# A graph and mixer block with routed experts: counts laid out by node, the mixer's sums taken over normalised x, the search before the statistics, the experts' tiles in the table's place

## Chip, cores and metric

The kernel runs on 1 core of one Trainium2 chip. The metric is the device time of the whole program in microseconds (us). Before the change it is 1842.44 us, the median of 4 runs (1831.82 to 1848.07).

## The reference, cut to what matters

```python
edge_index = jnp.stack([src, dst])                    # 200,000 edges, sorted by dst; 6,250 nodes, 256 channels
xn = _layernorm(x, axis=-1)
x = x + _L0_gnn_ref(edge_index, xn, W, b) \
      + _L0_mix_ref(xn[None], Wqkv, ln1_g, ln1_b, W1, b1, W2, b2, ln2_g, ln2_b)[0]
x = x + _L0_ffn_ref(_layernorm(x, axis=-1)[None], gate_w, gate_b, w1, b1, w2, b2)[0]

# _L0_gnn_ref: relu( sum over edges of (xn @ W)[src] * dinv[src] * dinv[dst], summed by dst, with self loops, + b )
# _L0_mix_ref: linear attention, 8 heads of 32
q, k = elu(q) + 1, elu(k) + 1
kv   = einsum('nshd,nshm->nhmd', k, v);  ksum = sum(k, axis=1)
z    = 1 / (einsum('nlhd,nhd->nlh', q, ksum) + 1e-6)
t    = einsum('nlhd,nhmd,nlh->nlhm', q, kv, z)
x1   = layer_norm(t + x) ; y = W2 gelu(W1 x1 + b1) + b2 ; layer_norm(y + x1)
# _L0_ffn_ref: softmax gate, top 1 of 8 experts, 977 slots per expert,
#              relu(h @ w1 + b1) @ w2 + b2, times the gate's probability
```

## The kernel before, in words

P is 128 and nodes are handled in NB = 49 tiles of 128 rows (the last has 106). The program has three stages, and the order of instructions on each engine is written out by hand in the first two: generators yield, and a loop takes turns between them.

**First stage.** Two generators alternate, `first_passes` (F) and `first_chain` (C); F may take FIRST = 0.79 steps for each step of C. Before the loop, the statistics of the first eight tiles of x are taken (`all_of(x_stats(8))`).
- C begins with `search()` (L424): 25 comparisons `lt` of the sorted dst list with node numbers, each with two matmuls into `et_ps` (L436), give a rough position for every eighth node; windows `er` of dst are then fetched and counted to find where each node's edges begin. Then come the statistics of the rest of x, `graph_rows` (which writes the scaled x as the table `tab` in SBUF and as `g_dram` in DRAM), interleaved with `edge_lists` (per-edge lists `idx`, `hiT`, `loT`), and `checked()`, which sums violations of the layout's assumptions into `odd`.
- F runs the mixer's first half over 25 groups of two tiles: x is normalised (`normed`, L682), transposed on PE (`turned`, L242), multiplied with Wq (L708), and with Wk and Wv together (L721, one bank of 512 columns a tile); ACT takes exp and relu of q and k and copies v with a column of ones into `va` (L730). `outer` (L694) sums k^T [v, 1] of each head pair into `kv_ps` with 129 columns. q goes to `q_dram`. Each group also writes a part of `xbuf` with zeros (`blanks`). F yields five times a group.
- At the end `kv_ps` is masked into `kvb`, `odd` is summed, `badi` is read by all engines (L766), and a branch (L767) leads to a general path that these inputs do not take.

**Main loop** (L871 on). Three generators alternate, driven by the gather's steps:
- `gather()`: for 18 tiles of nodes (GTS), edges are fetched by an indirect DMA of 128 rows of `g_dram` into `gt` (L977, GB = 9 buffers, issued LAG = 7 steps before use), and a matmul with a one-hot matrix `oh` sums them by node (L995).
- `dense()`: for the other 31 tiles (DTS; one of them called a block u), one-hot matrices `lo` and `hi` of the edges (DVE, L899) are multiplied on PE (L963) into counts `bp`: for each node pair of a step, 98 columns, how many edges go to it from each of the 49 source tiles. ACT casts the counts to bytes (L965) into `A`, laid out as [source row, source tile s, node]; 13 steps (NS) fill one A. In the block after, A is cast by source tile to `A_r` (L926; two buffers, four or five source tiles in each of 12 steps) and multiplied with the table, `ps_d` (L952). The sum goes through `put_sum` (L886).
- `rounds()`: for each group of two tiles the attention's result, the two layer norms, the MLP, the gate and the routing, in steps spread over three groups a, b and c; the norms run on ACT at L1199 with `nb` and `rs` from DVE's chain of small instructions (L222 to L1193). The tokens' rows go to `xbuf` by indirect DMA (L1076): 256 channels normalised, 256 as residual, the gate's probability and the row number, ROW = 514 floats.

**Experts** (L1307 on). For each of 8 experts `prepare` loads `w1e`, `w2e` and the expert's rows `xe` from `xbuf`, all issued on SP, and transposes them; `group` multiplies (L1360, L1370), scales by the probability `xe[:, i, 512]`, adds the residual and scatters rows to `out`. Its tiles are in a pool of their own, opened after the main loop's pools close.

The code before the change, where the two counts' casts stand:

```python
                s0, s1 = share(p)
                o = parts[p] = de.tile([P, 5, P], FR, name="A_r", tag="A_r")
                nc.scalar.copy(o[:, :s1 - s0, :], mats[u][:, s0:s1, :])
...
                        nc.scalar.copy(mats[u][:, :, GN * g0:GN * g1].rearrange("p s (g k) -> p g s k", k=GN),
                                       bp[:, :(g1 - g0) * HI].rearrange("p (g s k) -> p g s k", g=g1 - g0, k=GN))
```

Of the kernel before, what the change touches and what calls it, by code (L numbers as in the profile page):

```python
# [7 lines left out]
F32 = mybir.dt.float32  # L8
# [43 lines left out]
GB = 9  # L52
LAG = 7
# [3 lines left out]
FIRST = 0.79  # L57
# [12 lines left out]
def graph_block_kernel(  # L70
# [36 lines left out]

    main = ExitStack()
# [4 lines left out]
    big = main.enter_context(tc.tile_pool(name="big", bufs=1))  # L113
# [202 lines left out]
    vas = []  # L316
    for i in range(2):
        va = raw.tile([P, 2, 129], F32, name=f"va{i}")
        V.memset(va[:, :, 128:129], 1.0)
        vas.append(va)  # L320
# [32 lines left out]
    kv_ps = kps.tile([P, 2, 132], F32, name="kv_ps")  # L353
    cr_ps = rps.tile([P, 512], F32, name="cr_ps")
    sm_ps = rps.tile([P, 512], F32, name="sm_ps")
# [147 lines left out]
    def edge_lists():  # L503
# [38 lines left out]
        def ask(c):  # L542
            if c < NGC:
                got[c] = [rw.tile([P, P], I32, name=o, tag=o) for o in ("gd", "gs")]
                fetch(got[c], gsi[:, c:c + 1])
            elif c < NGC + NDC:
                d = 2 * (c - NGC)
                got[c] = [rw.tile([P, 2, P], I32, name=o, tag=o) for o in ("wd", "ws")]
                for h in range(2):
                    fetch([w[:, h, :] for w in got[c]], ei[:, d + h:d + h + 1])  # L550
# [28 lines left out]
        for c in range(NDC):  # L579
# [12 lines left out]
            V.scalar_tensor_tensor(kf, hs, float(GN), kf, op0=OP.mult, op1=OP.add)  # L592
# [70 lines left out]
    def first_passes():  # L663
# [11 lines left out]
        def normed(gi):  # L675
# [3 lines left out]
            xn = pair("S", 2, "xn")  # L679
            for i in range(n):  # L680
                v = xts[gi][:r, i, :] if gi >= NX else x_in(t0 + i, 1)[:, 0, :]
                nc.scalar.activation(xn[:r, i, :], v, AF.Identity,  # L682
# [9 lines left out]
        def outer(t, r, ek, va):  # L692
            for g in range(2):
                nc.tensor.matmul(kv_ps[:, g, :129], ek[:r, g * P:(g + 1) * P], va[:r, g, :],  # L694
                                 start=(t == 0 and g == 0), stop=(t == NB - 1 and g == 1))

        turned(0, normed(0))
        yield
        for gi in range(NGR):
# [12 lines left out]
            re = pair("G", 3, "re")  # L712
            nc.scalar.activation(re[:, :, :nn], qp[:, :, :nn], AF.Relu)
            xn = normed(gi + 1) if gi + 1 < NGR else None
            yield
            V.scalar_tensor_tensor(ex[:, :, :nn], ex[:, :, :nn], 1.0, re[:, :, :nn], op0=OP.min, op1=OP.add)
            nc.sync.dma_start(q_dram[gi, :, :, :nn], ex[:, :, :nn])
            for i in range(n):
                kp = bank()
                for c in range(2):  # L720
                    nc.tensor.matmul(kp[:r, :], xnt[:, c, i * r:i * r + r], wqkv_s[:, c, D:3 * D],  # L721
                                     start=(c == 0), stop=(c == 1))
                if late:
                    outer(*late.pop())
                ek = rw.tile([P, D], F32, name="ek", tag="ek", bufs=2)
                nc.scalar.activation(ek[:r], kp[:r, :D], AF.Exp)
                rk = rw.tile([P, D], F32, name="rk", tag="rk", bufs=1)
                nc.scalar.activation(rk[:r], kp[:r, :D], AF.Relu)
                va = vas[i]
                nc.scalar.copy(va[:r, :, 0:128], kp[:r, D:].rearrange("p (g m) -> p g m", g=2))  # L730
                yield
                V.scalar_tensor_tensor(ek[:r], ek[:r], 1.0, rk[:r], op0=OP.min, op1=OP.add)
                if i == 0 and xn is not None:
                    turned(gi + 1, xn)
                late.append((t0 + i, r, ek, va))
                yield
# [5 lines left out]
    with tc.manual_schedule():  # L742
        all_of(x_stats(8))
        F, C = first_passes(), first_chain()
        f = c = 0
        live = [True, True]
        while any(live):
            if live[1]:
                live[1] = next(C, "end") != "end"
                c += 1  # L750
            while live[0] and (f < FIRST * c or not live[1]):
                live[0] = next(F, "end") != "end"
                f += 1
        for g in range(2):
            V.tensor_tensor(kvb[:, g, 0:128], kv_ps[:, g, 0:128], hmask.rearrange("p a b -> p (a b)"), op=OP.mult)
            V.tensor_scalar(kvb[:, g, 128:132], hmask[:, :, 0], kv_ps[:, g, 128:129], None, op0=OP.mult)
# [5 lines left out]
        V.tensor_scalar(badi, bad, 0.5, None, op0=OP.is_gt)  # L762
    rwx.close()


    flag = nc.values_load(badi[0:1, 0:1], min_val=0, max_val=1)  # L766
# [102 lines left out]


    with tc.tile_pool(name="ga", bufs=GB, side="right") as ga, \  # L871
# [42 lines left out]
        def dense():  # L914

            mats, parts = {}, {}
            acc_ps = None

# [3 lines left out]
            def widened(u, p):  # L922

                s0, s1 = share(p)
                o = parts[p] = de.tile([P, 5, P], FR, name="A_r", tag="A_r")
                nc.scalar.copy(o[:, :s1 - s0, :], mats[u][:, s0:s1, :])  # L926
# [15 lines left out]
            for u in range(ND + 1):  # L942
                for p in range(NS):
                    k = u * NS + p
                    if u >= 1 and p >= 1:
# [4 lines left out]
                        A, (s0, s1) = parts.pop(p), share(p)  # L950
                        for hi in range(s0, s1):
                            nc.tensor.matmul(acc_ps, A[:, hi - s0, :], source(hi), start=False, stop=(hi == NB - 1))  # L952
                    make(k + 2)
                    if u < ND and p == 0:
                        mats[u] = de.tile([P, NB, P], U8, name="A", tag="A")
                    if u >= 1 and p < NS - 1:
                        widened(u - 1, p + 1)
                    if u < ND:
# [3 lines left out]
                        for g in range(g1 - g0):  # L962
                            nc.tensor.matmul(bp[:, g * HI:(g + 1) * HI], lo[:, g, :], hi[:, g, :],  # L963
                                             start=(g == 0), stop=(g == g1 - g0 - 1))
                        nc.scalar.copy(mats[u][:, :, GN * g0:GN * g1].rearrange("p s (g k) -> p g s k", k=GN),  # L965
                                       bp[:, :(g1 - g0) * HI].rearrange("p (g s k) -> p g s k", g=g1 - g0, k=GN))
# [116 lines left out]
        def rounds():  # L1083
# [3 lines left out]
            order = [NGR - 1] + list(range(NGR - 1))  # L1087
            xts, qs, ss, slots = {}, {}, {}, {}
# [4 lines left out]

            def load(k):
                if k < NGR:
                    gi = order[k]
                    t0, n = twos[gi]
                    r = rows(t0)
                    xts[gi] = pair("X", 3, "xt")
                    nc.sync.dma_start(xts[gi][:r, :n, :], node_rows(x, t0, n))  # L1100
                    qs[gi] = pair("Q", 2, "q")
                    nc.sync.dma_start(qs[gi][:, :, :n * r], q_dram[gi, :, :, :n * r])
# [11 lines left out]
            load(0)  # L1114
            yield
            for k in range(-2, NGR):
# [70 lines left out]
                if a is not None:  # L1187
                    load(k + 3)
# [104 lines left out]
        j = 0  # L1293
        while any(alive.values()):
# [4 lines left out]
            while alive["s"] and done_s < SIDE * (j + 1):  # L1299
                step("s", S)  # L1300
                done_s += 1
            j += 1
# [4 lines left out]
    with tc.tile_pool(name="fw", bufs=2) as fw, tc.tile_pool(name="fc", bufs=1) as fc, \  # L1307
# [14 lines left out]
        def prepare(e):  # L1322

            w1e = fw.tile([P, 2, DFF], F32, name="w1e", tag="w1e")
            nc.sync.dma_start(w1e, fw1[e].rearrange("(c p) f -> p c f", p=P))
            w2e = fw.tile([P, DFF // P, D], F32, name="w2e", tag="w2e")
            nc.sync.dma_start(w2e, fw2[e].rearrange("(c p) d -> p c d", p=P))
            xe = fw.tile([P, NCT, ROW], F32, name="xe", tag="xe")
            r0 = e * CAP
            for i0, i1 in ((0, 4), (4, NCT - 1)):  # L1330
                nc.sync.dma_start(xe[:, i0:i1, :],
                                  xbuf[r0 + i0 * P:r0 + i1 * P, :].rearrange("(t p) d -> p t d", p=P))
            nc.sync.dma_start(xe[:last, NCT - 1, :], xbuf[r0 + (NCT - 1) * P:r0 + CAP, :])
# [110 lines left out]
```

## Time and profile before

| | us |
|---|---|
| median of 4 runs | 1842.44 (1831.82 to 1848.07) |
| the profiled execution, whole | 1833.91 |
| its span, first to last instruction | 1832.0 |
| PE busy | 1495.7 (82%) |
| ACT busy | 1112.7 (61%) |
| DVE busy | 1087.6 (59%) |
| POOL busy | 775.3 (42%) |
| mean granted clock of TensorE | 0.919 |
| DMA | 286.43 MB, 156 GB/s over the span |

PE is the matmul unit, PEld its weight loads, DVE the vector engine, ACT the scalar engine, POOL GpSimd, SP the engine that issues most DMAs. "L952" is line 952 of the kernel. In a line of groups the name before the arrow is the tile written, those after it the tiles read; then shape, count, busy time, mean ns of one, and the idle time of the engine just before it with what ended it. In the order of time each line has start, duration, engine, line, tile, count and in brackets the idle time before it and its releaser. In a line of waits come the total, the number of times and the longest. Durations of pipelined instructions overlap, so the time from start to next start is the one that adds up.

### The profile page before, as it was taken

The numbers are of one execution on the slowest core, as the hardware profiler recorded it, in microseconds if no ns is written. First come the engines' busy times: TensorE is split into PE (matmuls) and PEld (weight loads), VectorE is DVE, ScalarE is ACT, GpSimd is POOL, SyncE is SP. The second block draws the span as 40 slices with busy tenths as digits, with TensorE's granted clock in tenths as the row PEclk, the third lists the DMA queues.
The fourth block names the chain that finished last, engine by engine and source line by source line (L and its number), as shares of the span: only waits on it lengthen the run. The fifth ranks groups of instructions, "written<-read, shape, count | busy, mean of one in ns | idle before, by whom it ended". The sixth has DMA issues, their size and how long they took to land. (4 is left out here: it accounts for less than half of the span.)

```text
span 1832.0 us, 23628 instructions
## 1 busy us (share of the span) xinstructions
PE 1495.7 (82%) x7678; PEld 1062.5 (58%) x7678; DVE 1087.6 (59%) x3430; ACT 1112.7 (61%) x1794; POOL 775.3 (42%) x771
## 2 busy tenths in 40 slices
PE   4887776888878888888788888877888649999997
PEld 2555454665556665556665565555666426777775
DVE  4765856675676677667676767666866412323323
ACT  1844656777676877677777777776777313233332
POOL 0104506556546565555565556555565311111111
PEclk9988996999989998989888999988999969999999
DMA  7546787666556666565666666655566462332330
GB/s 227 153 121 196 256 256 190 162 162 175 147 158 167 157 168 176 145 167 150 160 171 166 161 165 165 167 142 159 154 170 155 109 218 104 108 107 103 111 107 21
DMA packets 184987, 286.43 MB, mean 156 GB/s; under 512 B 28457, under 2 KB 78564, under 8 KB 184714
## 3 DMA queue, kind: packets, MB, share of 16 engines
q0 software_dynamic: 96304, 180.15, 37.7%
q1 hardware_dynamic: 88250, 103.44, 17.4%
q8 instruction: 70, 1.15, 0.3%
q10 hardware_dynamic: 288, 1.08, 0.1%
q14 instruction: 75, 0.61, 0.1%
HBM read 226.90 MB, written 60.39 MB: 157 GB/s over the span
## 5 line engine op out<-in xcount | busy, mean ns | idle before, releaser
L977 POOL DMA_INDIRECT gt<-g_dram,idxc x612 | 624.1, 1020 | 524.8 <-PE ps L995 298.0
L965 ACT CAST A<-bp 128x490 uint8<-128x490 f32 (+1 forms) x403 | 511.7, 1272 | 259.3 <-PE bp L963 116.6
L952 PE MATMUL ps_d<-tab,A_r 128*128 128x512 f32 x1519 | 468.0, 434 | 118.9 <-ACT A_r L926 92.2
L952 PEld LDWEIGHTS ps_d<-tab,A_r 128*128 128x128 f32 x1519 | 297.7, 205 | 224.1 <-ACT A_r L926 123.0
L995 PE MATMUL ps<-gt,oh 128*128 128x512 f32 x612 | 280.2, 492 | 9.4 <-DMA gt<-g_dram,idxc 8.8
L899 DVE TENSOR_TENSOR lo<-rowb,lo 128x640 bf16<-128x640 bf16 (+1 forms) x403 | 194.1, 482 | 126.7 <-PE bp L963 44.8
L926 ACT CAST A_r<-A 128x512 fp32r<-128x512 uint8 x372 | 251.5, 676 | 15.7 <-PE ps_d L952 5.7
L963 PEld LDWEIGHTS <-lo 128*128 128x128 bf16 x1984 | 107.7, 104 | 130.3 <-issue 65.4
L963 PE MATMUL bp<-hi,lo 128*128 128x98 bf16 x1984 | 168.9, 218 | 12.5 <-DVE hi L899 9.8
L1388 POOL DMA_INDIRECT out<-rep,who x43 | 42.5, 988 | 300.4 <-DVE rep L1386 201.9
L986 DVE TENSOR_TENSOR oh<-rowb,rel 128x256 fp32r<-128x256 bf16 x306 | 127.7, 418 | 68.7 <-PE ps L995 35.7
L899 DVE TENSOR_TENSOR hi<-hib,hi 128x490 bf16<-128x490 bf16 (+1 forms) x403 | 162.9, 404 | 0.0
L1360 PE MATMUL hpf<-xet,w1e 128*128 128x512 f32 (+2 forms) x544 | 151.5, 436 | 5.6 <-ACTq L1400 3.5
L1370 PE MATMUL ypf<-w2e,hm 128*128 128x256 f32 (+1 forms) x688 | 151.3, 379 | 0.0
L1370 PEld LDWEIGHTS ypf<-w2e,hm 128*128 128x128 f32 (+1 forms) x688 | 128.9, 188 | 21.9 <-issue 3.1
L995 PEld LDWEIGHTS ps<-gt,oh 128*128 128x128 f32 x612 | 114.9, 203 | 16.0 <-DMA gt<-g_dram,idxc 8.2
L1360 PEld LDWEIGHTS hpf<-xet,w1e 128*128 128x128 f32 x544 | 85.5, 191 | 65.3 <-issue 57.4
L1362 ACT ACTIVATE hm<-hpf,fb_s 128x512 f32<-128x512 f32 (+2 forms) x136 | 71.1, 526 | 78.3 <-PE hpf L1360 72.9
L1372 DVE TENSOR_TENSOR y<-ypf,fb_s 128x256 f32<-128x256 f32 (+1 forms) x43 | 18.2, 423 | 142.8 <-PE ypf L1370 142.8
L721 PE MATMUL mm<-wqkv_s,xnt 128*128 128x512 f32 (+1 forms) x196 | 97.7, 623 | 0.0
L1373 ACT ACTIVATE y<-y,xe 128x256 f32<-128x256 f32 (+1 forms) x43 | 21.8, 508 | 119.4 <-DVE y L1372 119.4
L1076 POOL DMA_INDIRECT xbuf<-slot,put x48 | 52.8, 1101 | 61.3 <-issue 50.5
(307 smaller groups left out, 2035.6 us busy)
## 6 DMA issues: line engine op xcount, KB each, us to landing
g_dram<-tab SPq DMA_DIRECT2D x24, 512.0 KB
xt<-in_x SPq DMA_DIRECT2D x42, 256.0 KB
xbuf<-zeros SPq DMA_DIRECT2D x26, 384.0 KB
gt<-g_dram,idxc POOLq DMA_INDIRECT x612
xe<-xbuf SPq DMA_DIRECT2D x8, 1028.0 KB
w1e<-in_fw SPq DMA_DIRECT2D x8, 1024.0 KB
w2e<-in_fw SPq DMA_DIRECT2D x8, 1024.0 KB
xe<-xbuf SPq DMA_DIRECT2D x8, 771.0 KB
```

Source lines behind the costliest of these rows:

```text
L721: nc.tensor.matmul(kp[:r, :], xnt[:, c, i * r:i * r + r], wqkv_s[:, c, D:3 * D], start=(c == 0), stop=(c == 1))
L899: V.tensor_tensor(one[:, :g1 - g0, :].rearrange("p g (w t) -> p g w t", t=2), row.rearrange("p (w t) -> p w t", t=2).unsqueeze(1).to_broad ...
L926: nc.scalar.copy(o[:, :s1 - s0, :], mats[u][:, s0:s1, :])
L952: nc.tensor.matmul(acc_ps, A[:, hi - s0, :], source(hi), start=False, stop=(hi == NB - 1))
L963: nc.tensor.matmul(bp[:, g * HI:(g + 1) * HI], lo[:, g, :], hi[:, g, :], start=(g == 0), stop=(g == g1 - g0 - 1))
L965: nc.scalar.copy(mats[u][:, :, GN * g0:GN * g1].rearrange("p s (g k) -> p g s k", k=GN), bp[:, :(g1 - g0) * HI].rearrange("p (g s k) -> p ...
L977: nc.gpsimd.indirect_dma_start(out=gt, out_offset=None, in_=g_dram, in_offset=bass.IndirectOffsetOnAxis(ap=idxs[j // IC][:, j % IC:j % IC ...
L986: V.tensor_tensor(oh, rowb.unsqueeze(1).to_broadcast([P, 2, P]), rel[:, m:m + 2].unsqueeze(2).to_broadcast([P, 2, P]), op=OP.is_equal)
L995: nc.tensor.matmul(ps, ohs.pop(i), tiles.pop(i), start=False, stop=(e == EB - 1))
L1360: nc.tensor.matmul(hp[:, :nn], w1e[:, c, f * P:(f + 1) * P], xet[:, c, at:at + nn], start=(c == 0), stop=(c == 1))
L1362: nc.scalar.activation(hm[:, f, :nn], hp[:, :nn], AF.Relu, bias=fb1_s[:, e * 8 + f:e * 8 + f + 1])
L1370: nc.tensor.matmul(yp[:r, :], hm[:, f, (i - i0) * P:(i - i0) * P + r], w2e[:, f, :], start=(f == 0), stop=(f == DFF // P - 1))
```

## The change

- **Counts by node.** `A` is laid out as [source row, node, source tile]. The cast of `bp` writes in a row; the cast to `A_r` reads with a step of 49 bytes, in chunks of CH = 7 source tiles (7 a block instead of 12).
- **GB and LAG** go from 9 and 7 to 8 and 6.
- **Mixer.** `xn` gets a column of ones and three buffers of its own; k is computed for both tiles of a group in one bank, with no v; `outer` sums k^T [xn, 1] with 257 columns into `kx_ps` (two banks). After the loop `kx` is copied, transposed and multiplied with Wv into kv, and then masked. `normed` runs two groups ahead. Three yields a group; FIRST is 0.465. `sm_ps` becomes a part of the bank of `cr_ps`.
- **Search ahead.** ALONE = 9 steps of C run before `all_of(x_stats(8))`.
- **Flag.** `judged()` sums `odd` when C ends, and `badi` is read two steps of F later; the branch stands where it stood.
- **Rounds' first loads** of x and q are issued before the branch.
- **Experts in the table's place.** The pool `big` of the tables stays open to the end. The experts' weights lie in T0 and T1, `xe` in T2 and T3, `hm` in T4 and T5. The first expert's weights are asked for as soon as gather and dense are through, while rounds still runs. `xe` has 512 columns; probability and row number come as `xm` by DMAs of their own; the first expert's first four tiles come one by one. Both halves of a transposed group are written before the copies.
- hi's index becomes node times 49 plus source tile: `kf * NB + hs` in place of `hs * GN + kf`.

```diff
-GB = 9
-LAG = 7
+GB = 8
+LAG = 6
...
+ALONE = 9
+FIRST = 0.465
...
-            V.scalar_tensor_tensor(kf, hs, float(GN), kf, op0=OP.mult, op1=OP.add)
+            V.scalar_tensor_tensor(kf, kf, float(NB), hs, op0=OP.mult, op1=OP.add)
...
-            for i in range(n):
-                kp = bank()
...
-                    nc.tensor.matmul(kp[:r, :], xnt[:, c, i * r:i * r + r], wqkv_s[:, c, D:3 * D],
+            kp = bank().rearrange("p (t o) -> p t o", t=2)
+            for i in range(n):
...
+                    nc.tensor.matmul(kp[:r, i, :], xnt[:, c, i * r:i * r + r], wqkv_s[:, c, D:2 * D],
...
+                    nc.tensor.matmul(kx_ps[:, g, :D + 1], ek[:r, i, g * P:(g + 1) * P], xns[gi % 3][:r, i, :],
...
+        for _ in range(ALONE):
+            next(C)
+        all_of(x_stats(8))
...
+                if not live[1]:
+                    badi = judged()
+                    asked = f + 2
...
+                if not live[1] and f == asked:
+                    flag = nc.values_load(badi[0:1, 0:1], min_val=0, max_val=1)
...
+        kx = pair("S", 2, "kx")
+        nc.scalar.copy(kx, kx_ps[:, :, :D])
...
+                nc.tensor.transpose(tp[:, (2 * c + g) * P:(2 * c + g + 1) * P], kx[:, g, c * P:(c + 1) * P], ident)
...
+                nc.tensor.matmul(kv[:, g * P:(g + 1) * P], kxt[:, c, g, :], wqkv_s[:, c, 2 * D + g * P:2 * D + (g + 1) * P],
...
+            CH = 7
...
+            def widened(u, c):
+                if 0 <= u < ND and c * CH < NB:
+                    o = parts[u, c] = de.tile([P, CH, P], FR, name="A_r", tag="A_r")
+                    nc.scalar.copy(o, mats[u][:, :, c * CH:(c + 1) * CH].rearrange("p n s -> p s n"))
...
-                        mats[u] = de.tile([P, NB, P], U8, name="A", tag="A")
-                    if u >= 1 and p < NS - 1:
-                        widened(u - 1, p + 1)
+                        mats[u] = de.tile([P, P, NB], U8, name="A", tag="A")
+                    if p >= 1:
+                        for hi in range(*share(p)):
+                            if hi and hi % CH == 0:
+                                widened(u - 1, hi // CH + 1)
...
+                        nc.scalar.copy(mats[u][:, GN * g0:GN * g1, :].rearrange("p n s -> p (n s)"), bp[:, :(g1 - g0) * HI])
+                    if p == NS - 1:
+                        widened(u, 0)
+                    if p == 0:
+                        widened(u - 1, 1)
...
+            if not (alive["g"] or alive["d"] or weights):
+                weights.append(weights_of(0))
...
-            xe = fw.tile([P, NCT, ROW], F32, name="xe", tag="xe")
+            xe = big.tile([P, NCT, 2 * D], F32, name="xe", tag=f"T{2 + e % 2}")
+            xm = fw.tile([P, NCT, 2], F32, name="xm", tag="xm")
...
-            hm = fw.tile([P, DFF // P, 512], F32, name="hm", tag="hm")
+            hm = big.tile([P, DFF // P, 512], F32, name="hm", tag=f"T{4 + len(hms) % 2}")
```

## The prediction

> **What bounds the kernel now.** I first cut the span into its stages with the busy time by stretch (columns: length; busy time and count for PE, PEld, DVE, ACT, POOL; granted clock; DMA share; GB/s).
>
> ```profile
> 0.00:276.00 276.00, 204.88 (x828) 129.39 (x828) 181.30 (x635) 142.99 (x367) 54.23 (x67) 0.93 0.65 201
> 276.00:1457.00 1181.00, 967.34 (x5462) 698.55 (x5462) 800.68 (x2513) 858.94 (x1212) 672.94 (x656) 0.91 0.61 161
> 1457.00:1499.00 42.00, 9.28 (x38) 7.10 (x38) 11.04 (x55) 3.12 (x7) 5.62 (x5) 0.59 0.57 199
> 1499.00:1832.00 333.00, 314.17 (x1352) 227.50 (x1352) 94.60 (x228) 107.64 (x210) 42.50 (x43) 0.99 0.28 96
> ```
>
> The main loop is 1181 of 1832 us, and no engine fills it: PE 82%, ACT 73%, DVE 68%, POOL 57%. The experts are PE throughout (94%). So I next asked, for 300 to 1420, whom PE waits for, and then for ACT's groups by shape:
>
> ```profile
> PE ps_d L952 <- ACT A_r L926: 86.9, 45, 7.8
> ```
>
> ```profile
> L965 ACT CAST A<-bp 128x490 uint8<-128x490 f32 x359 | 463.3, 1290 | 230.1 <-PE bp L963 99.7 <-remote 62.7 <-PE ps L995 55.1
> L926 ACT CAST A_r<-A 128x512 fp32r<-128x512 uint8 x330 | 220.9, 669 | 0.6
> L926 ACT CAST A_r<-A 128x640 fp32r<-128x640 uint8 x29 | 22.4, 771 | 0.0
> ```
>
> PE and ACT wait for each other in turn. The order of time shows how:
>
> ```profile
> 833.67 0.63 ACT L926 CAST A_r<-A 128x512 fp32r<-128x512 uint8 x1
> 834.19 1.30 ACT L965 CAST A<-bp 128x490 uint8<-128x490 f32 x1
> ...
> 834.36 1.20 PE L952 MATMUL ps_d<-tab,A_r 128*128 128x512 f32 x4
> ...
> 838.36 1.09 ACT L1199 ACTIVATE s<-s,nb,rs 128x256 f32<-128x256 f32 x2 [2.86 <-DVE nb L1193]
> ...
> 840.34 0.60 ACT L926 CAST A_r<-A 128x512 fp32r<-128x512 uint8 x1
> ...
> 840.99 2.08 PE L952 MATMUL ps_d<-tab,A_r 128*128 128x512 f32 x4 [4.89 <-ACT A_r L926]
> ```
>
> The next A_r is queued on ACT behind two layer norms (838.36 to 840.34), the first of which waits 2.86 us for DVE; PE idles 4.89 us and then runs four matmuls in 2.08 us instead of 1.20, at a clock of 0.50 from 841 to 845.
>
> **Counts by node.** *Cast.* It read 490 floats and wrote pairs of bytes 128 apart; from start to next start it takes about 1.02 us (830.49 to 831.51). Now it writes 490 bytes in a row, as A_r does now: 0.52 us a 512 (833.67 to 834.19), slope (771-669)/128 = 0.80 ns an element, so 0.50 us. *Widening.* 7 chunks of 896 a block instead of 12 of about 512, each element now read 49 bytes on. In a row 896 would take 0.52 + 384 x 0.80 = 0.83 us; what the step adds, no ACT row shows. The cast bounds it above: its write lost 0.52 us on 490 elements, 1.06 ns an element or 2.12 ns a jump (245 jumps). The nearest read is on DVE, 256 bytes a step:
>
> ```profile
> L428 DVE CAST lastf<-dl x1: 186/186/186, 22.1 to 22.1; 125x25 f32<-125x25 int32 x1
> ```
>
> ```profile
> L493 DVE COPY begin<-cr_ps x1: 210/210/210, 105.5 to 105.5; 128x49 f32<-128x49 f32 x1
> ```
>
> ```profile
> L528 DVE COPY picked<-sm_ps x2: 169/172/175, 147.8 to 149.1; 128x16 f32<-128x16 f32 x2
> ```
>
> 16 and 49 elements in a row take 172 and 210 ns, so 25 would take 182; the strided read took 186, 0.16 ns an element more. A gain below a row of 0.83 us is excluded: the count of elements is the same. So a chunk takes 0.97 (DVE's price), 1.78 (the write's mean) or 2.73 us (the write's jump). I take 0.5 ns, nearer to the read: 1.28 us.
>
> [...]
>
> A block was 13 x 1.02 + 12 x 0.52 = 19.5 us of ACT and becomes 13 x 0.50 + 7 x 1.28 = 15.5. Over 31 blocks ACT gives back 124 us (192 at DVE's price, 16 at the write's mean, minus 189 at its jump). What PE gets: in 300 to 1420 it idles 196 us, of which about 125 name ACT (A_r 86.9, norms and copies the rest). Waits of ACT on DVE's `nb` and `rs` chain, 34 us, stay, since rounds() is untouched. Over the longer loop I take 85 us. The clock's loss is 0.09 x 1181 = 106 us; with 85 of some 206 us of idle gone, I take 20 of it, half of its part. **Loop: -105** (-150 to +75).
>
> [...]
>
> What is late next: POOL needs 612 x (0.94+0.30) + 48 x 1.4 = 826 us, DVE 801, both under 1076. GB 8 and LAG 6 leave six steps of 1.74 us, 10.4 us; the third gather was issued at 279.71 and used at 285.04, so 5.3 us: cost nothing, and if a tile came late each wait would cost what the 10 waits for gt cost now, 9 us in all. A_r keeps two buffers: a chunk waits for the last matmul on the one two before it, as now, and the cast queued behind it waits with it, as now.
>
> **Mixer.** In PE's order of time:
>
> ```profile
> 114.36 1.88 PE L721 MATMUL mm<-wqkv_s,xnt 128*128 128x512 f32 x4
> 116.08 0.61 PE L694 MATMUL kv_ps<-va,ek 128*128 128x129 f32 x4
> 116.52 1.89 PE L708 MATMUL mm<-xnt,wqkv_s 128*128 128x256 f32 x8
> 118.25 1.88 PE L721 MATMUL mm<-wqkv_s,xnt 128*128 128x512 f32 x4
> ```
>
> A tile's keys and values take 1.72 and the outer product 0.44 us. L708's eight rows are four products of 256 columns in 1.73 us; a tile's keys are now two of those, 0.87, and its outer product, two of 257, the same: 1.74 instead of 2.16, 0.42 x 49 = 21 us of PE. ACT loses a copy a tile and two starts a group, about 0.6 x 25 = 15 us. PE is full in 50 to 70, 100 to 165 and 230 to 262, about half of the stage, so 10 us count there, and 2 elsewhere. **-12** (0 to -21). New at the end are a copy, four transposes, a copy, eight product rows and the masks: 0.6 + 1.1 + 0.6 + 0.9 + 0.3, with handovers +4.5.
>
> **Search ahead, flag, rounds' loads.** The first matmul waits until 22.80 now, while dst is the first load queued and DVE idles from about 6 to 15.3. 25 compares of 0.42 us with two products each (0.49 us) pass there; x's statistics (6.8 us) then start near 20 instead of 15.3, but 12.2 us of search on PE leave the mixer's way: **-8** (-16 to +5). The flag's stop is 269.25 to 275.97 now. Its read moves among the last groups: each engine still stops to read it, with the last two groups of the mixer queued behind it on PE and ACT and the last blank fills on SP, so I count 4.5 of the 6.7 us as hidden, which the new end chain takes: **0** (-3 to +4.5). Loads of x and q issued before the branch, behind those fills: -1. Stage: -21. The cover that could fail is DMA: 0.91 busy in 230 to 262; then the -12 is gone.
>
> **Experts in the table's place.** Weights for two experts are queued when the tables are last read, about 1457, not at 1471.7; on SP one `out` store and the xe loads stand behind them. The last scatter (1484.70) landed only by 1491.24 beside these 4 MB; I take -4, and -2 for the first xe by tiles: **-6** (0 to -12). Eight-byte xm rows lie beside 40 us of PE per expert: 0 (+8 if the first scale had to wait for them). Transposes and matmuls are as many: 0.
>
> Sum: -105 - 21 - 6 = -132 on 1833.9 (span 1832.0 and 1.9 around it): 1702. The median of runs is 8.5 above that execution: **1710**.
>
> **Rivals.** (1) *Slower:* the strided read costs the write's jump, 2.73 us a chunk. ACT then has 859 + 189 = 1048 us in the loop; busy at the 82% that PE reaches now, it takes 1278, +97; with some slack taken up +75, less 27: 1890. Break-even of ACT is 1.86 us a chunk; above about 2.2 it decides. For it: 2.12 ns a jump in L965. Against: 0.16 ns in DVE's read. 0.10. (2) *The coupling stays:* ACT is faster but bursts still wait for `nb`, and PE keeps two thirds of its idle: loop -40, total 1775; at the write's mean price it would be near 1800. For it: the 4.89 us above. 0.18. (3) *The change does not reach the path:* the first stage runs on DMA and the loop on DVE's and PE's order: -15 or less, 1842 within 1%. 0.05. (4) *PE nearly full:* the loop loses nearly all of PE's 196 us of idle, -185: 1630. 0.05. The forecast has the rest, 0.62, alone 1645 to 1760.
>
> The range must leave out at most 0.2: below 1640 lies 0.05, above 1805 the 0.10 and 0.05: 1640 to 1805. One per cent is what a measurement here can tell from no change: faster 0.85, same 0.05, slower 0.10.
>
> **What would show it.** A cast near 0.6 us and A_r chunks of 1.0 to 1.6 us; above 2.2, rival 1. PE's wait for A_r under 45 us and a loop near 1075. The search done by 25 us, the loop begun near 255. If A_r is short and the loop still near 1140, rival 2 holds; if the first stage stays at 276, DMA does.

## Result and profile after

The changed kernel takes 1839.59 us (median of 34 runs, 1827.1 to 1853.8); the kernel before, run beside it, 1839.4 us (55 runs). The ratio is 1.0006, 95% interval 0.9991 to 1.002: no change. The forecast was 1710. The profiled execution has a span of 1837.9 us against 1832.0.

First the stages, by stretch, cut as before (columns as there):

```profile
0.00:276.00 276.00, 189.55 (x845) 150.82 (x845) 180.58 (x621) 129.79 (x273) 56.92 (x70) 0.88 0.66 204
276.00:1457.00 1181.00, 972.58 (x5455) 719.35 (x5456) 798.73 (x2505) 784.97 (x1055) 669.49 (x654) 0.89 0.62 163
1457.00:1499.00 42.00, 11.93 (x39) 7.27 (x38) 10.99 (x54) 2.73 (x6) 5.63 (x5) 0.54 0.40 135
1499.00:1837.90 338.90, 315.82 (x1352) 228.10 (x1352) 92.68 (x221) 108.07 (x211) 42.48 (x43) 0.98 0.30 96
```

The same cuts still fit: no stage became shorter by more than a few us. In the main loop ACT lost 74 us of busy time (858.9 to 785.0) and PE is as busy as before (972.6, 967.3). In the first stage PE lost 15 us of busy time, and the counts' first product starts 2.9 us earlier (274.31, was 277.17). The experts are 6 us longer. Now ACT's two casts by shape, and whom PE waits for between 300 and 1420 ("issue" is idle time in which an engine waited for nothing that the profile shows):

```profile
L981 ACT CAST A_r<-A 128x896 fp32r<-128x896 uint8 x217 | 390.8, 1801 | 81.0 <-PE ps_d L1006 50.3 <-PE ps L1056 16.2 <-remote 8.2
L1023 ACT CAST A<-bp 128x490 uint8<-128x490 f32 x372 | 206.0, 568 | 181.3 <-PE bp L1021 90.2 <-remote 37.6 <-PE ps L1056 29.1
```

```profile
PE mm L243 <- ACT s L1248: 34.6, 18, 4.3
PE ps_d L1006 <- ACT A_r L981: 27.0, 20, 4.1
PE mm L1110 <- DVE fore L1106: 24.0, 9, 3.5
PE mm L243 <- issue: 22.8, 15, 4.6
PE bp L1021 <- issue: 17.7, 7, 4.8
PE mm L243 <- DVE ag L940: 12.9, 8, 3.5
PE mm L1209 <- ACT agt L1182: 11.6, 7, 3.4
PE mm L1280 <- ACT x1t L1262: 9.4, 6, 2.5
```

And before, beside the wait for A_r shown in the prediction:

```profile
PE mm L242 <- ACT s L1199: 19.7, 14, 3.9
PE mm L1049 <- DVE fore L1045: 16.3, 7, 3.2
```

The cast became 0.57 us, as forecast (near 0.6). A piece of A_r takes 1.80 us, outside the forecast's 1.0 to 1.6. PE's wait for A_r went from 86.9 to 27.0 us, below the 45 of the forecast, and PE idles as long as before all the same: 1120 - 926.7 = 193 us of 1120, 196 before. The idle time has other names, those of the rounds: the normalised s (34.6, was 19.7), fore (24.0, was 16.3), x1t (9.4, was 2.4).

### The profile page after: what moved, and what is told of

The parts are those of the page before. It is cut to its first block, busy times and chain, and to the rows that moved or that the text cites. A ratio compares the mean times of both kernels' runs of the same rounds, so it can differ in the third digit from the quotient of the medians.

```text
span 1837.9 us, 23460 instructions
## 1 busy us (share of the span) xinstructions
PE 1489.9 (81%) x7690; PEld 1105.5 (60%) x7690; DVE 1083.0 (59%) x3399; ACT 1025.6 (56%) x1544; POOL 774.5 (42%) x771
## 5 line engine op out<-in xcount | busy, mean ns | idle before, releaser
L1006 PE MATMUL ps_d<-tab,A_r 128*128 128x512 f32 x1519 | 457.4, 425 | 36.5 <-ACT A_r L981 30.5
L981 ACT CAST A_r<-A 128x896 fp32r<-128x896 uint8 x217 | 390.8, 1801 | 81.0 <-PE ps_d L1006 50.3
L1006 PEld LDWEIGHTS ps_d<-tab,A_r 128*128 128x128 f32 x1519 | 310.5, 206 | 116.5 <-ACT A_r L981 43.9
L1023 ACT CAST A<-bp 128x490 uint8<-128x490 f32 (+1 forms) x403 | 220.9, 561 | 234.9 <-PE bp L1021 115.8
L1056 PE MATMUL ps<-gt,oh 128*128 128x512 f32 x612 | 287.3, 505 | 5.2 <-DMA gt<-g_dram,idxc 4.6
L1416 PE MATMUL hpf<-xet,w_e 128*128 128x512 f32 (+2 forms) x544 | 154.2, 441 | 8.9 <-ACTq L1457 3.5
L1426 PE MATMUL ypf<-w_e,hm 128*128 128x256 f32 (+1 forms) x688 | 151.6, 379 | 0.0
L1426 PEld LDWEIGHTS ypf<-w_e,hm 128*128 128x128 f32 (+1 forms) x688 | 128.8, 188 | 22.2 <-issue 3.8
L1416 PEld LDWEIGHTS hpf<-xet,w_e 128*128 128x128 f32 x544 | 86.6, 193 | 70.7 <-issue 62.4
L1056 PEld LDWEIGHTS ps<-gt,oh 128*128 128x128 f32 x612 | 118.5, 209 | 11.0 <-DMA gt<-g_dram,idxc 6.4
L1429 ACT ACTIVATE y<-y,xm 128x256 f32<-128x256 f32 (+1 forms) x43 | 21.8, 508 | 134.7 <-DVE y L1428 134.7
L1248 ACT ACTIVATE s<-s,nb,rs 128x256 f32<-128x256 f32 (+1 forms) x98 | 53.5, 594 | 61.8 <-DVE nb L1242 30.9
```

Source lines behind the costliest of these rows:

```text
L981: nc.scalar.copy(o, mats[u][:, :, c * CH:(c + 1) * CH].rearrange("p n s -> p s n"))
L1006: nc.tensor.matmul(acc_ps, parts[u - 1, hi // CH][:, hi % CH, :], source(hi), start=False, stop=(hi == NB - 1))
L1023: nc.scalar.copy(mats[u][:, GN * g0:GN * g1, :].rearrange("p n s -> p (n s)"), bp[:, :(g1 - g0) * HI])
L1056: nc.tensor.matmul(ps, ohs.pop(i), tiles.pop(i), start=False, stop=(e == EB - 1))
L1416: nc.tensor.matmul(hp[:, :nn], w1e[:, c, f * P:(f + 1) * P], xet[:, c, at:at + nn], start=(c == 0), stop=(c == 1))
L1426: nc.tensor.matmul(yp[:r, :], hm[:, f, (i - i0) * P:(i - i0) * P + r], w2e[:, f, :], start=(f == 0), stop=(f == DFF // P - 1))
```

## Experiments

**Two levels of chips.** The kernel before takes 1839 us on the chips of the result and 1840 on the one of e9 to e12, but 1730 to 1732 on those of e1 to e8 and e13 to e18. Absolute times are compared only within a level; ratios are to the kernel before on the same chip. Each chip was used in one stretch of time only, so chip and hour are not told apart.

To place gains, the spans below are cut at the starts of the gather's products (L995 before, L1056 after) as the trace has them: the 51st, the 601st and the 612th, the last. Each row is one profiled execution, and whole times of one kernel spread (the kernel before by 16 us over 27 runs on e5's chip), so a few us in a stretch are not a finding by themselves. "The loop" below is the stretch from the 51st to the 601st product, if nothing else is said.

| | ratio (95%) | to the 51st | 51st to 601st | 601st to 612th | to the end |
|---|---|---|---|---|---|
| before, result's chip | 1 | 371.3 | 1061.8 | 23.5 | 375.2 |
| changed, result's chip | 1.0006 (0.9991 to 1.002) | 371.1 | 1065.3 | 21.2 | 380.3 |
| e6 before | 1 | 357.5 | 980.0 | 16.9 | 375.2 |
| e5 changed | 1.0045 (1.0025 to 1.0065) | 358.2 | 974.1 | 22.0 | 384.9 |
| e7 before, GB 8, LAG 6 | 1.0074 (1.0045 to 1.0104) | 358.0 | 993.2 | 16.4 | 377.5 |
| e8 before, by node, GB 8 | 1.0021 (0.9997 to 1.0045) | 358.9 | 977.1 | 15.4 | 377.4 |
| e2 changed, old counts | 1.0165 (1.0138 to 1.0192) | 360.1 | 996.5 | 22.8 | 385.4 |
| e4 changed, short casts | 1.0023 (1.0001 to 1.0046) | 356.6 | 969.7 | 21.9 | 383.9 |
| e1 changed, read in a row | 0.9859 (0.9829 to 0.9889) | 355.2 | 942.8 | 22.6 | 381.3 |
| e3 changed, norms wait for nothing | 0.9876 (0.9829 to 0.9923) | 353.7 | 900.9 | 19.3 | 427.1 |
| e15 before, by node, GB 9, norms later, half on DVE | 1.0377 (1.0342 to 1.0413) | 360.1 | 1040.1 | 16.1 | 384.8 |
| e13 changed, GB 9 | 0.9955 (0.9937 to 0.9973) | 358.9 | 958.5 | 23.8 | 385.8 |
| e14 before, norms later | 0.9842 (0.9802 to 0.9882) | 359.2 | 946.3 | 17.2 | 378.9 |
| e16 changed, GB 9, norms later | 0.9757 (0.9723 to 0.9791) | 351.7 | 933.3 | 22.6 | 386.1 |
| e17 e16, code moved | 0.9755 (0.9726 to 0.9784) | 351.7 | 933.3 | 21.4 | 375.6 |
| e18 e17, norms later again | 0.9705 (0.9677 to 0.9733) | 347.6 | 926.0 | 19.2 | 379.8 |
| e9 changed, code moved (slower level) | 1.0002 (0.9976 to 1.0028) | 366.9 | 1076.4 | 19.2 | 377.1 |
| e10 changed, loads once (slower level) | 1.0057 (1.0027 to 1.0086) | 376.9 | 1068.4 | 21.2 | 383.8 |
| e11 before, by node, GB 9 (slower level) | 0.9909 (0.9885 to 0.9934) | 377.3 | 1048.8 | 22.5 | 377.2 |
| e12 e11, norms later (slower level) | 0.985 (0.9826 to 0.9875) | 375.1 | 1043.0 | 20.3 | 375.4 |

The theories after the result were: (1) the strided cast's price holds ACT, and ACT holds PE; (2) PE's idle comes from hand-overs between engines in their fixed order, the rounds' norms above all, so a lighter ACT only renames it; (3) the clock takes back what idle is saved.

**e1: the read in a row.**

```diff
-nc.scalar.copy(o, mats[u][:, :, c * CH:(c + 1) * CH].rearrange("p n s -> p s n"))
+nc.scalar.copy(o.rearrange("p s n -> p (s n)"), mats[u].rearrange("p n s -> p (n s)")[:, c * CH * P:(c + 1) * CH * P])
```

> The changed kernel, but the cast to A_r reads its 896 counts in a row instead of 49 bytes apart (so the counts are taken for other source tiles and the aggregates are other numbers); the number of casts and their size stay. Theory 1 (the step's price holds ACT and ACT holds PE): a cast of 896 falls from 1.80 to about 0.85-0.95 us, ACT gives back some 190 us, and the loop with it falls by 70 or more: total about 1760. Theory 2 (PE's idle in the loop is set by hand-overs between the engines in their fixed order, and a shorter cast only moves it to other waits): total 1815 to 1840, PE's idle between 300 and 1420 stays near 190 us under other names. Theory 3 (the clock takes back what idle is saved): idle falls, busy time of PE grows by as much, clock below 0.88.

ACT's group in e1, then what PE waits for between 300 and 1320, in e1 and after it in e5:

```profile
L981 ACT CAST A_r<-A 128x896 fp32r<-128x896 uint8 x217 | 204.3, 942 | 93.1 <-PE ps_d L1006 91.7
```

```profile
PE mm L243 <- ACT s L1248: 57.3, 30, 4.1
PE mm L1110 <- DVE fore L1106: 25.7, 11, 3.5
```

```profile
PE mm L243 <- ACT s L1248: 55.7, 34, 4.3
PE mm L1110 <- DVE fore L1106: 28.7, 11, 3.5
```

The same 896 elements take 0.94 us in a row and 1.80 at the step: the step costs 0.86 us a piece, 187 us of ACT over 217 pieces. Taking all of it away shortens the loop by 31 us (974.1 to 942.8), a sixth. The waits for s and fore stand as they were. Theory 1 is refuted as the main cause: the price is real, but little of ACT's work is on the path. Theory 2's number was missed too: it allowed a fall of 25 us at most. The clock was 0.92, not below 0.88, and PE's busy time in the loop fell together with its idle time (844 to 834 us, 130 to 109): theory 3 finds nothing here.

**e2, e7, e8, e13: layout against GB and LAG.** e2 puts the old counts into the changed kernel, e7 and e8 change the kernel before. e13 cuts A_r into pieces of 5:

```diff
-GB = 8
-LAG = 6
-            CH = 7
+GB = 9
+LAG = 7
+            CH = 5
...
-                        for hi in range(*share(p)):
-                            if hi and hi % CH == 0:
-                                widened(u - 1, hi // CH + 1)
+                    if p < NS - 1:
+                        for hi in range(*share(p + 1)):
+                            if hi % CH == 0:
+                                widened(u - 1, hi // CH)
```

> The changed kernel with the counts laid out as before (cast of 1.27 us in pairs of bytes, twelve A_r casts of about 0.67 us a block), everything else changed, GB 8 and LAG 6 too. If counts by node gave the loop nothing, the time stays at 1840 within 0.4%. If they gave some 40 us that another part of the change took back (GB and LAG, or the first stage), it rises to about 1880. If they cost time, it falls below 1830.

> The changed kernel unaltered, since the kernel before takes 1732 us on the chip of the experiments and 1839 on that of the result. If the chip only sets the level, the ratio is 1.000 within 0.004 here too. If the long waits that the profile calls issue and remote, which the runs of this chip do not show, hid a gain of the change, it is faster than the kernel before by 1% or more; e2 (1.0165 with the old counts) and e4 (1.002) then frame it.

> The kernel before unaltered, for its profile on this chip: 1732 us in all. The 107 us that it is faster than in the profile shown lie in the main loop if they come from PE's waits (loop near 1075 instead of 1181), and over all stages if they come from the clock.

> The kernel before with GB 8 and LAG 6 alone. e2, which differs from it by the new first stage and experts, is 1.0165 of the kernel before. If the shorter gather queue is what costs e2 its 28 us, this is at 1.01 or above, with PE waiting longer for gt; if it costs nothing (as predicted), 1.000 within 0.003.

> The kernel before with the counts laid out by node, and GB 8 and LAG 6, which its larger A_r needs; first stage, rounds' loads and experts as before. Beside e7 it gives the worth of the layout alone: theory 1 with a read at 1.80 us: 20 to 40 us below e7; theory 2: within 10 us of e7.

> The changed kernel with A_r in ten pieces of 5 source tiles asked for a step ahead, so that GB 9 and LAG 7 fit again (e11's loop in the changed kernel). If GB and LAG took the loop's gain back (e7: 13 us), it is 10 to 15 us below the changed kernel: 0.992 to 0.996 of the kernel before. If the other parts of the change hold the loop too, it stays within 5 us of the changed kernel.

The pair cancels. GB 8 and LAG 6 alone lengthen the loop by 13 us (e6 to e7; interval of the ratio clear of 1). The layout at equal GB gives 16 us (e7 to e8; 12 by the medians) and 22 in the changed kernel (e2 to e5). With both, the loop of the kernel before is 3 us shorter (e6 to e8), and the ratio, 1.0021, shows no gain. With nine buffers again, the changed kernel's loop falls by 16 us (e5 to e13) and its ratio from 1.0045 to 0.9955. e13 also cuts A_r into shorter pieces and asks for them earlier; e4, which does so with eight buffers, in still shorter pieces, gains 4 us. So A_r's larger pieces took a buffer from the gather, and that cost most of what the layout gave.

e7 and e8 also show the renaming. Whom PE waits for between 300 and 1320, in e7 and in e8, and then the loop of each (columns as in the stages):

```profile
PE ps_d L952 <- ACT A_r L926: 44.2, 42, 5.6
PE mm L242 <- ACT s L1199: 39.5, 24, 4.3
```

```profile
PE mm L242 <- ACT s L1206: 55.4, 29, 4.3
PE ps_d L952 <- ACT A_r L927: 2.7, 4, 1.1
```

```profile
357.96:1351.12 993.16, 862.48 (x4994) 627.94 (x4993) 727.45 (x2284) 783.64 (x1106) 607.55 (x590) 0.93 0.67 172
358.91:1336.00 977.09, 850.42 (x4994) 637.80 (x4993) 727.58 (x2284) 719.79 (x963) 606.16 (x591) 0.92 0.68 175
```

The layout takes 64 us of busy time from ACT and nearly all of PE's wait for A_r, yet PE's idle time over the same work only falls from 130.7 to 126.7 us. The other 12 us are shorter busy time of PE, at nearly the same clock; why is not shown.

Against what was expected, e7 (1.0074) and e2 (23 us above e5 by the medians, not 40) lie between their numbers, and so does e8, 12 us below e7. e5 just misses 1.000 within 0.004: it shows a small loss on this level of chips, where the result shows none. e13 came as expected, 13.5 us below e5. By e6, 82 of the 102 us of span between the levels lie between the 51st and the 601st product (1061.8 against 980.0).

**e4: short pieces in three buffers.** `CH = 4`, asked for a step ahead as in e13, GB 8 and LAG 6 kept.

> The changed kernel with the strided cast to A_r in 13 pieces of 4 source tiles in three buffers, each asked for one step before its use, when its buffer has been free for a step, instead of 7 pieces of 7 in two buffers, asked for in the step that frees the buffer. ACT's sum grows by about 13 x 1.05 - 7 x 1.70 = 1.8 us a block, 55 us in all; its waits for ps_d before A_r (50 us, of 5.7 in the kernel before) go. Theory 1: slower, about 1870. Theory 2 with the new head-of-line waits and the long pieces as its cause: faster, 1800 to 1825. Neither: within 10 us.

1.0023, an interval that overlaps e5's: neither theory's number, and within the 10 us of the last sentence. What ACT waits for in e4, by shape and then by releaser between 300 and 1320:

```profile
L982 ACT CAST A_r<-A 128x512 fp32r<-128x512 uint8 x372 | 414.3, 1115 | 2.1 <-PE ps_d L1007 1.3
```

```profile
ACT s L1244 <- DVE nb L1238: 72.6, 23, 4.8
```

The wait for A_r's buffers is gone (1.3 us; 65.9 in e5), and the wait for nb grew from 61.3 in e5 to 72.6. The loop is 4 us shorter, although ACT spends 22 us more on A_r (414.3 against 392.6 in e5). Removing those head-of-line waits brought at most little; how much the longer casts took back isn't separated.

**e11, e12: the kernel before with the layout, GB 9, and then later norms** (on the slower level of chips). e12 adds:

```diff
-SIDE = 1.25
+SIDE = 1.34
...
                 yield
                 yield
+                yield
+                yield
 
                 def norm(o, s, r, n, at):
```

> The kernel before with the counts by node, but A_r in ten pieces of 5 source tiles, which fit into the old buffers, so GB 9 and LAG 7 stay; each piece is asked for a step before its use. e7 gave GB and LAG 13 us of the loop, e8 minus e7 gave the layout 16. If both add up: 12 to 16 us below the kernel before, 0.992. If the shorter pieces take it back as in e4: 0.996 to 1.000.

> e11 with the rounds' norms two steps later than rs and nb (four empty yields instead of two) and SIDE 1.34 instead of 1.25, so that the rounds keep up. In e3 the loop fell by 73 us between the 50th and the 600th gather when the norms waited for nothing. If it is the wait of ACT in front of the norms, with the casts queued behind it, most of ACT's 50 us there goes and the total falls 25 us or more below e11. If the chain itself (norms, transposes, products) sets PE's waits wherever it stands, under 10 us.

e11 is 0.9909, as the sum of e7 and e8 said. e12 is 0.985: 11 us below e11, between the two sides' numbers, on a chip with stalls of its own (below).

**e3, e14, e16, e18: the wait in front of the norms.** e3 scales the norms with `nmr` and `rstd`, which lie ready; e14 puts e12's later norms into the kernel before, e16 into e13; e18 adds a fifth yield (SIDE 1.39).

> The changed kernel, with the rounds' layer norms scaled by x's own statistics, which lie ready since the first stage, instead of rs and nb (other numbers come out; DVE still works out rs and nb). ACT no longer waits for DVE's chain before the norms. Theory 2: PE's waits for the normalised s (35 us) and for fore go down and the total falls by 30 or more, to about 1805. Theory 1: ACT waits 50 us less in front of the norms but its casts hold PE; total down by under 15.

> The kernel before with only the norms two steps later and SIDE 1.34 (counts, GB and LAG as before). If the wait in front of the norms is a loss of its own, this wins the 10 us that e12 has over e11: 0.994. If it paid only because the casts had become shorter: 1.000 within 0.002.

> e13 with the norms two steps later and SIDE 1.34: what is left between this and e12 is the worth of the change's other parts (mixer, search, flag, experts in the table's place). By the profiles of e5 and e6 they cost 5 to 10 us: this is 5 to 10 us above e12.

> e17 with one step more between nb and the norms (five empty yields) and SIDE 1.39. In e16 ACT still waits 31 us for nb between 300 and 1320. If that wait is still PE's idle: 8 to 15 us below e17. If the one-hot matrices (27 us) and A_r (23 us) now end last: within 4 us of e17.

In e3 the loop falls by 73 us (974.1 to 900.9), more than from any cut of ACT's work; its experts take 42 us longer because other numbers are routed (768 hpf products in its trace, 544 in e5's), so the ratio understates it. e14 does no work less and gains 34 us in the loop, 1.6% in all, more than either side named. It also raises SIDE, the rounds' steps for each step of the gather, from 1.25 to 1.34, to make up for the two added steps of a round; SIDE alone was not run, but e3 leaves it at 1.25. What ACT and PE wait for between 300 and 1320, first ACT in e5, then both in the kernel before (e6) and in e14:

```profile
ACT s L1248 <- DVE nb L1242: 61.3, 23, 4.6
```

```profile
ACT s L1199 <- DVE nb L1193: 50.5, 23, 4.8
```

```profile
PE ps_d L952 <- ACT A_r L926: 45.0, 43, 6.3
PE mm L242 <- ACT s L1199: 36.9, 27, 3.7
```

```profile
ACT s L1201 <- DVE nb L1193: 13.6, 13, 2.5
```

```profile
PE mm L242 <- ACT s L1201: 13.0, 14, 2.4
PE ps_d L952 <- ACT A_r L926: 27.2, 40, 1.7
```

A wait of ACT for nb delays every cast queued behind it, A_r too: moving the norms cut PE's wait for A_r with A_r's price untouched. The gain is not only idle time. The loop in e6 and in e14:

```profile
357.53:1337.53 980.00, 853.67 (x4990) 621.18 (x4986) 724.32 (x2280) 781.49 (x1104) 606.58 (x589) 0.94 0.68 174
359.20:1305.54 946.34, 835.76 (x4990) 608.10 (x4986) 722.01 (x2278) 780.71 (x1104) 618.61 (x589) 0.97 0.70 180
```

For the same work PE idles 110.6 instead of 126.3 us, and is busy 18 us less, at a granted clock of 0.97 instead of 0.94. Theory 2 is shown, and its place is the norms behind nb.

e16 against e14 (0.9757, 0.9842) is the worth of the whole change once the norms and GB are out of the way: 0.85%. e16 was expected 5 to 10 us above e12; by the ratios it is 0.9% below (0.9757, 0.985), though e12 ran on the slower level. e18 wins another 10 us of median (1676.98 against 1686.71 us for e17), as expected if the wait still cost PE, with ACT's wait for nb at 15.8 us instead of 31.3 between 300 and 1300; 7 us of it are in the loop of the profiles. It is the fastest kernel of the study, 0.9705.

**e15: half of A_r on DVE**, in e12's kernel (`V.tensor_copy if c % 2 else nc.scalar.copy`).

> e12 with every second piece of A_r cast on DVE instead of ACT. ACT loses about 155 casts of 1.34 us, 190 us; DVE gains as many. If DVE reads the step of 49 bytes at the price of its strided reads in the profile (a piece of 640 in 0.8 to 1.0 us) and the loop hangs on ACT's load: 15 to 30 us below e12. If DVE's order (one-hot matrices, norm chain) is the tighter one: slower than e12.

```profile
L928 ACT CAST A_r<-A 128x640 fp32r<-128x640 uint8 x155 | 207.6, 1339 | 37.6 <-PE ps_d L953 36.7
L928 DVE CAST A_r<-A 128x640 fp32r<-128x640 uint8 x124 | 159.2, 1284 | 25.3 <-PE ps_d L953 25.0
```

1.0377: slower. DVE takes about as long for 640 bytes at the step, 1.28 us against ACT's 1.34, and its order is the tighter one: PE now waits 118.4 us for DVE's A_r between 300 and 1320. So the price is not ACT's alone; no run has DVE read these bytes in a row.

**e9, e17: the branches between the experts.** In the changed kernel's last stage PE stands still before one group of experts. In PE's order of time, changed kernel (result's chip), then the kernel before at the same place (e6):

```profile
1792.05 1.04 PE L1398 MATMUL tpf<-ident,xe 128*128 128x128 f32 x8
1793.74 1.11 PE L1398 MATMUL tpf<-ident,xe 128*128 128x128 f32 x8 [0.66 <-ACT xet L1402]
1798.29 16.17 PE L1416 MATMUL hpf<-xet,w_e 128*128 128x512 f32 x32 [3.44 <-PEq L1455]
```

```profile
1690.92 0.62 PE L1344 MATMUL tpf<-ident,xe 128*128 128x128 f32 x4 [0.26 <-ACT xet L1347]
1692.22 14.00 PE L1360 MATMUL hpf<-xet,w1e 128*128 128x512 f32 x32 [0.68 <-ACTq L1398]
```

PEq L1455 is PE's branch over the groups that this expert does not need. The trace has it at 3.74 us in the changed kernel (1794.24 to 1797.98), 0.45 in the kernel before on the same chip; two reads of the instruction queues (16 KB at 1795.23, 8 KB at 1797.24) fall into the long one. The 32 products after the pause take 16.17 us instead of 14.00, and the granted clock is 0.50 from 1798 to 1802. A second long branch (3.52 us) stands before the end. e9 and e17 add, ahead of the search, where PE has nothing to do:

```diff
+        dummy = bank()
+        for _ in range(10):
+            nc.tensor.matmul(dummy[:, :P], ident, ident, start=True, stop=True)
```

> The changed kernel with ten products of ident with itself added before the search, where PE has nothing to do (their result is not used). They move PE's program by 41 instructions, so that the branch after the last but one group of experts lies where the kernel before has it (17,555th instruction instead of 17,514th; 17,556th before). If the 3.4 to 3.8 us that this branch takes in the changed kernel, of 0.35 to 0.45 in the kernel before, is fetching code from a place set by the program's layout, it takes under 1 us here, PE's wait before the last hpf goes, and the total falls by 5 to 7 us. If it comes from the experts' weights or tiles in the table's place, it stays.

> e16 with the ten unused products of e9, which bring the branches between the experts back to where the kernel before has them (14,733rd and 17,558th instruction of PE; e12 and e14 have the same places and no long branch, e16 has two of 3.4 and 3.8 us and one of 1.3). If the branches cost what PE then waits and runs at half clock, the stretch from the last gather to the end falls from 386 to 376 us and the ratio from 0.976 to about 0.970; if only the branch's own time shifts, 0.976.

By their profiles the branch takes 0.45 us in both. At the same place e17 shows:

```profile
1642.81 1.11 PE L1399 MATMUL tpf<-ident,xe 128*128 128x128 f32 x8 [0.66 <-ACT xet L1403]
1644.60 5.85 PE L1417 MATMUL hpf<-xet,w_e 128*128 128x512 f32 x13 [0.68 <-ACTq L1456]
```

In the profiles the stretch to the end falls from 386.1 (e16) to 375.6 us (e17), with loops of 933.3 us each: by the profiles the changed kernel's loss in the experts goes with the long branches, and moving the code removes them here. In the whole times it isn't settled: medians 1691.15 and 1686.71 us, ratios 0.9757 and 0.9755, and e9 at 1.0002 (0.9976 to 1.0028) shows no fall against the changed kernel's 1.0006. e18 has its branches where the kernel before has them and one of them takes 3.76 us: the place in the program alone doesn't decide it. What does is open.

**e10: the rounds' first loads once.** The changed kernel issues them in two loops (L791, L809); e10 drops the second.

> The changed kernel without the second of its two loops that load the rounds' first x and q (both issue the same loads, 1 MB again). In e5 PE starts on the counts 6 us earlier than in e6, then waits 6.1 us for q, and after 50 gathers both stand at 358 us. If the repeated loads hold up the first q, the wait falls under 2 us and the 50th gather is used near 353; total down by 3 to 6 us. If the start is set by the gather's own first transfers, it stays at 358.

The wait for q is gone (PE waits 6.7 us for ht instead), but the 51st product starts at 376.9 us and the ratio is 1.0057 (1.0027 to 1.0086): taking the repeated loads away does not bring the start forward. The changed kernel itself was not run on this chip; e9, which was, has 366.9 and a median 8 us lower. Why e10 is slower isn't explained.

## Why the prediction was wrong, step by step

The term that failed is the loop's, -105: measured on one level of chips it is -6 (e5 against e6), on the other +3.5. Three steps of it failed: the price of a widening piece, the share of ACT's time that PE gets, and GB and LAG at nothing. The sign that was named for success, PE's wait for A_r under 45 us, came true (27.0) without the gain.

- **Widening.** Of the three prices, which go from start to start, the middle one (the write's mean, 1.78 us) was near: 1.69 is measured (809.90 to 811.59 below). I took 1.28 because a DVE read of 25 elements at a step cost 0.16 ns an element more. By the rows of 16 and 49 elements (172 and 210 ns) some 154 of its 186 ns don't depend on the count, an estimate; it reads four-byte numbers and the rows beside it read PSUM tiles, so it can't price 896 bytes; DVE itself takes 1.28 us for 640 in e15. In order of time in the changed kernel:

```profile
809.44 0.57 ACT L1023 CAST A<-bp 128x490 uint8<-128x490 f32 x1
809.90 1.79 ACT L981 CAST A_r<-A 128x896 fp32r<-128x896 uint8 x1
811.59 0.57 ACT L1023 CAST A<-bp 128x490 uint8<-128x490 f32 x1
```

  From start to start 0.46 and 1.69 us: a block is 13 x 0.46 + 7 x 1.69 = 17.8 us of ACT instead of 19.5, 52 us over 31 blocks where 124 were forecast.
- **What PE gets.** I let PE have 85 of 124 us (0.69), plus 20 from the clock. Measured: 16 us of loop for e8's layout, which gives ACT about 52 by the sum above (0.3; 64 and 0.25 by the loop's busy time), and 31 for e1's 187 (0.17). Of e8's 16 us only 4 are idle time of PE. The 20 us from the clock did not come (0.91 before, 0.89 after in the stage of the loop). Rival 2 named this mechanism; its price, -40, was still too kind, as it went with cheap reads and free GB. The waits on nb and rs that I left standing at 34 us were the lever: moving the norms brought 34 us of loop (e14). That the two numbers are equal is chance: in e14 ACT's wait for nb fell by 37 us, PE's idle time by 16, and its busy time by 18 at a higher clock.
- **GB and LAG.** "Cost nothing" was wrong: 13 us (e7). I had taken the 5.3 us from issue to use of one early tile for all of them. PE's wait for gt in the whole span is 15.8 us in e7 and 5.5 in e6.
- **First stage, -21.** PE's work fell by 15 us and the counts' first product starts 6.1 us earlier (275.5 in e6, 269.4 in e5), but by the 51st product both stand at 358. The search's last product came at 28.8 us (was 45.4, forecast 25), but the stage did not follow PE: on the result's chip PE's idle time before 276 grew from 71 to 86 us as its work fell, with longer waits on DVE's chain (wd 7.6 to 15.3 us, pick 5.6 to 12.5, between 40 and 262). With later norms a gain is there at the 51st product: 351.7 in e16 against 359.2 in e14, about a third of the forecast.
- **Experts, -6.** The first transposes start 1.0 us earlier (1394.6 in e6, 1393.6 in e5), and the last gathers run 5 us longer (16.9 to 22.0); no run separates why. After the last gather the changed kernel loses 9.7 us, most of it at the branches by the profiles of e16 and e17. I had costed this part's transfers, and not the code's new place.
- **Outcome.** e5 against e6: +0.7 - 5.9 + 5.1 + 9.7 = 9.6 us of span, where -132 was forecast. The chance of "same", 0.05, belonged to rival 3, a change off the path; what happened is a change whose gain in the loop was small to begin with, and was eaten by its own buffer and, by the profiles, by its own code.

## What to carry to other kernels

Where several engines wait for each other in a fixed order, first find the wait that stands at the head of an in-order queue (here the norms behind nb) and move it; taking work off the engine behind it brought a sixth to a third of that work here. Price a strided access by a row with as many elements of the same width: 25 elements on DVE showed 0.16 ns an element for their step, 896 bytes on ACT 0.96 for theirs (1.80 against 0.94 us). A wait that disappears by name is no gain yet: compare the waiting engine's idle and busy time over the same work. When a tile grows, ask which buffer paid for it, and compare with that buffer given back.

## What the hardware showed that was not expected

- The chips of these runs stood on two levels, 1730 and 1839 us for the same kernel. Single products differ little: those of ps_d took 420 ns in the mean in e6 and 434 in the profile before. Of the 82 us more in the loop of the kernel before, 58 are idle time of PE (184 against 126 us) and 24 busy time, at a clock of 0.92 against 0.94. The slower level shows waits that the profile calls remote (58 us of ACT before the counts' cast, between 300 and 1320), which e6 does not show, and PE's wait for A_r is twice as long (86.9 and 45.0). In e12, on the slower level, all engines and their rows in order of time:

```profile
694.44 0.57 ACT L969 CAST A<-bp 128x490 uint8<-128x490 f32 x1 [6.02 <-remote]
694.44 0.49 DVE L899 TENSOR_TENSOR lo<-rowb,lo 128x640 bf16<-128x640 bf16 x1 [1.32 <-remote]
...
696.65 1.22 PE L953 MATMUL ps_d<-tab,A_r 128*128 128x512 f32 x2 [6.21 <-issue]
```

  PE's last product before it ended at 690.4 by the profile; ACT and DVE, which wait for PE, both go on at 694.44. Why, is open.
- On the result's chip a branch of PE between the experts took 0.07 to 0.91 us in the kernel before and 0.07 to 0.46 in the changed kernel, but for two there (3.74 and 3.52). PE's wait at the first of these is 3.44 us, 3.57 in e5, and the 32 products after it take 2 us more (16.17 against 14.00).
- A read of bytes at a step of 49 took ACT and DVE about 2 ns an element (1.34 and 1.28 us for 640 in e15); in a row ACT took 0.94 us for 896 (e1).
